# A top-p attention kernel on one core: one bound's trial moved to VectorE, pauses between ScalarE's trials, q in three parts

## The chip, the cores and the metric

The kernel runs on one core of one Trainium2 chip. A core has five engines, each with its own queue of instructions taken in order: TensorE (PE, matrix products), VectorE (DVE), ScalarE (ACT, functions of one input), GpSimd (POOL) and SyncE (SP, here only transfers). Engines wait for each other by semaphores. The metric is the device time of one execution in microseconds (us); lower is better.

## What is computed

A graph layer (layer 0) and an attention layer (layer 1) on 3327 nodes of 256 features. The change lies in layer 1:

```python
def _top_p_attention(X, W1, W2, W3):
    q = X @ W1.T @ W2.T
    k = X @ W3.T
    probs = softmax(q @ k.T)
    idx = argsort(-probs)
    sp = take_along_axis(probs, idx)
    cs = cumsum(sp)
    keep_sorted = cs - sp < 0.9
    mask = zeros(probs.shape).at[rows, idx].set(keep_sorted)
    A = probs * mask
    return A / maximum(A.sum(-1, keepdims=True), 1e-12)

for n in range(2):
    A = _top_p_attention(Xa, W1, W2, W3)
    Xf = R @ Xf
    Xa = A @ Xa
    Z = Z + Xf @ U1[n].T + Xa @ U2[n].T
h = X + Z
return layernorm(h) * ln_g + ln_b
```

R is the neighbours' average with the node itself. For each row the attention keeps the largest probabilities until their sum reaches 0.9.

## The kernel before

**Tiles and items.** The 3327 rows are 26 tiles of 128 (the last has 127). Layer 1 runs 52 items: step 0's tiles, then step 1's; item i covers one tile. An item's product (`product`) is seven groups: `turn` transposes four 128x128 blocks of the masked probabilities on TensorE (L1403) and copies them to SBUF on ScalarE (L1405, `at`); `times` multiplies them with Xa (L1419, `pav`). Between the groups lie seven slots, into which `run` puts the work of other items: logits (L1196, L1199), exponentials, the sorted lists on VectorE, the mask (L1320). `scaled` (L1430) divides by the row's sum. The order of TensorE, ScalarE and VectorE is thus written by hand: an engine takes its instructions in the order in which the calls stand. GpSimd's and SyncE's order is left to a scheduler.

**Extra tiles.** Most rows find their threshold in a sorted list of their 72 largest probabilities. Rows that do not are put aside: `put_aside_1` and `put_aside_2` give them numbers and scatter their index, offset and sum to a table (L1529 on VectorE, L1530 on GpSimd). They are done again in three extra tiles h0, h1, h2 of 128 rows each. For each:

- `hard_load` fetches the rows' numbers (`payh`, L1542 and L1543 cast them) and gathers their features (L1551; in the last item six gathers: three of h2, and the fourth source, Xf after the second step, of each extra tile).
- `hard_q` makes q: transposes (L1180), a copy (L1182, `xtqh`), two matmuls (L1562, `pqh`), a copy (L1564), then a first bound `top` of the threshold (L1570, L1571).
- `hard_exp` makes the probabilities in four pairs of pieces: matmuls (L1581, `plh`) and exponentials (L1584).
- The bound of the threshold is then lowered by up to six trials, at a factor of 1/16, 1/4, 1/2, 0.71, 0.84 and 0.92 (`CUTS`). A trial sums what lies above a candidate and asks whether it still reaches the needed mass. `coarse_bound` does a trial on ScalarE: four activations over half of the row each (L1601), then eight small operations on GpSimd (L1607 to L1616, and L1596 of the next trial). `bound` does one on VectorE: the candidate (L1628), one instruction over 128x3327 (`kept_sum`, L1340), two small ones.
- `hard` sums what lies below the bound (L1643), lists and sorts it, and masks the probabilities (L1672). `hard_end` is the product of the extra tile, in four parts.

**The end.** After the last product, `ends` runs in ticks (`more`). In each tick the next step of an extra tile's product or start is taken, one of the 26 normal tiles' ends is begun (`tile_end`), and every open one goes a stage further: transposes and copies two ticks later (L1180, L1182 `xtut`, `xtvt`), output terms three ticks later (L1439), then the copy (L1447), and two layer norms (L1392 to L1394) and the store. Below, te0 to te25 are these ends; te_k's terms come in tick k + 3. At the close of a tick, the open coarse bounds are given two steps:

```python
            for _ in range(2):
                for g in bounds:
                    if not next(g, True):
                        break
```

Two steps are one pair of activations. `hard(0)` drives ticks 1 to 8, h1's trials on VectorE 9 to 11, `hard(1)` 12 to 19; the product of h0 lies in ticks 9 to 12.

**Where the extra tiles' work stands before.** q of h0 stands in slot 6 of item 48, q of h1 in slot 3 of item 50 (`total` is 52). h0's first trial on ScalarE lies in item 50, its second in the last item, slots 0 and 1; its other four on VectorE in slots 2 to 6 of the last item. h1's first trial on ScalarE lies in slots 3 to 6 of the last item, its second and third in ticks 1 to 4. `start(2)` makes q and the exponentials of h2; its three trials on ScalarE follow in ticks 5 to 10.

Of the kernel before, what the change touches and what calls it, by code (L numbers as in the profile page):

```python
# [17 lines left out]
N = 3327  # L18
# [56 lines left out]
CUTS = tuple(2.0 ** -f for f in (4.0, 2.0, 1.0, 0.5, 0.25, 0.125))  # L75
# [1046 lines left out]
class Layer1:  # L1122
# [432 lines left out]
        )  # L1555

    def hard_q(self, k):
        nc, v = self.nc, self.items[f"h{k}"]
        xt = self.transposed((v.x[:, 0, :],), P, f"q{v.tag}")
        pq = self.psm.tile([P, 512], F32, tag="sm", name=f"pq{v.tag}")  # L1560
        for c in range(DC):
            nc.tensor.matmul(pq[:, :P], self.sh.wq[:, c, :], xt[:, c, :], start=(c == 0), stop=(c == DC - 1))  # L1562
        v.q = self.work.tile([P, DC, P], F32, tag="xtq", name=f"q{v.tag}")[:, 0, :]
        nc.scalar.copy(v.q, pq[:, :P])  # L1564

        v.p = (*self.more, self.p[0])[k]
        v.other = (self.l[0][:, :N], self.l[1][:, :N], self.p[1])[k]

        v.top = self.small(f"top{k}", f"top{v.tag}")
        nc.scalar.activation(v.top, v.pay[:, 3:4], AF.Exp, bias=v.pay[:, 1:2])  # L1570
        nc.gpsimd.tensor_scalar(v.top, v.top, 1.0001, None, ALU.mult)  # L1571
# [14 lines left out]
    def coarse_bound(self, k, cuts, junk):  # L1586


        nc, v = self.nc, self.items[f"h{k}"]
        tag = v.tag  # L1590
        less = self.small(f"less{k}", f"less{tag}")
        nc.gpsimd.tensor_scalar(less, v.pay[:, 2:3], 0.5 * (1.0 - 1e-5), None, ALU.mult)
        for f in cuts:
            tag = f"{v.tag}_{f}"
            minus = self.small(f"minus{k}", f"minus{tag}")
            nc.gpsimd.tensor_scalar(minus, v.top, -f, None, ALU.mult)  # L1596
            s = self.small(f"sums{k}", f"sums4{tag}", 4)
            for h in range(2):
                on = slice(h * HALF, min(N, (h + 1) * HALF))
                for j, func in enumerate((AF.Relu, AF.Sign)):  # L1600
                    nc.scalar.activation(  # L1601
                        junk[:, on], v.p[:, on], func, bias=minus, accum_out=s[:, 2 * h + j : 2 * h + j + 1]
                    )
                    if h == 0 or j == 0:
                        yield
            both = self.small("both", f"both{tag}", 2)
            nc.gpsimd.tensor_tensor(both, s[:, 0:2], s[:, 2:4], ALU.add)  # L1607
            number = self.small("many4", f"many4{tag}")
            nc.gpsimd.tensor_scalar(number, both[:, 1:2], 0.5, 0.5 * N, ALU.mult, ALU.add)
            nc.gpsimd.tensor_tensor(number, number, minus, ALU.mult)  # L1610
            nc.gpsimd.tensor_tensor(number, both[:, 0:1], number, ALU.subtract)
            up = self.small("up4", f"up4{tag}")
            nc.gpsimd.tensor_scalar(up, number, less, f - 1.0, ALU.is_lt, ALU.mult)
            nc.gpsimd.tensor_scalar(up, up, 1.0, None, ALU.add)
            nxt = self.small(f"top{k}", f"top{tag}")
            nc.gpsimd.tensor_tensor(nxt, up, v.top, ALU.mult)  # L1616
            v.top = nxt
            yield

    def bound(self, k, cuts):  # L1620
# [122 lines left out]
    def ends(self, bounds):  # L1743


        ends, open_ends, queue = [self.tile_end(t) for t in range(NT)], [], []

        def tick():

            if ends:  # L1750
                open_ends.append(ends.pop(0))
            for g in list(open_ends):
                if next(g, True):
                    open_ends.remove(g)

        def more():
            if queue and next(queue[0], True):
                queue.pop(0)
            tick()
# [4 lines that stand above are left out]
                        break  # L1764

        def start(k):
            self.hard_q(k)
            for pair in self.chunks():
                yield
                self.hard_exp(k, pair)  # L1770
            bounds.append(self.coarse_bound(k, CUTS[:COARSE], self.items[f"h{k}"].other))

        def end(k):
            yield from self.hard_end(k)
            open_ends.append(self.items[f"h{k}"].end)

        queue.append(start(2))
        for k in range(HARD):
            if k:
                for _ in bounds[k - 1]:  # L1780
                    pass
                for _ in self.bound(k, CUTS[COARSE:]):
                    more()
            for _ in self.hard(k):
                more()
            queue.append(end(k))
        while queue or open_ends or ends:
            more()
        for k in range(HARD):
            self.hard_store(k)  # L1790

    def run(self):
        nc, sh, total = self.nc, self.sh, STEPS * NT
        self.items = {}
        with self.tc.manual_schedule(
# [14 lines left out]
            for i in range(total):  # L1810
# [8 lines left out]
                def slot(g, f, *a):  # L1819
                    slots[g].append(lambda: f(*a))  # L1820
# [28 lines left out]
                if i == NT + CLOSE + 1:  # L1849
                    slot(0, self.hard_load, 0)  # L1850
                    slot(0, self.hard_load, 1)
                if i == total - 4:
                    slot(6, self.hard_q, 0)
                if i == total - 2:
                    slot(3, self.hard_q, 1)
                for k, at, first in ((0, total - 3, 0), (1, total - 2, 3)):
                    if i == at:
                        for j, pair in enumerate(self.chunks()):
                            slot(first + j, self.hard_exp, k, pair)

                if total - 2 <= i:
                    coarse = self.coarse_bound(0, CUTS[i - total + 2 :][:1], self.l[0][:, :N])
                    for g in (0, 1, 2, 3) if i == total - 2 else (0, 0, 1, 1):
                        slot(g, next, coarse, None)
                for k, pair in enumerate(pairs):
                    slot(2 * k, self.some_logits, i + 2, pair, end)
# [1 line left out]
                    slot(g, next, rest, None)  # L1868
                if i + 1 == total:
                    self.put_aside_2(i)  # L1870
                    bound = self.bound(0, CUTS[2:])
                    bounds = [self.coarse_bound(1, CUTS[:COARSE], self.l[1][:, :N])]
                    for g in (2, 3, 4, 5, 6):
                        slot(g, next, bound, None)
                    for g in (3, 4, 5, 6):
                        slot(g, next, bounds[0], None)
                    slot(5, self.hard_load, 2)
                    for k in range(HARD):
                        slot(5, self.hard_gather, k, 3, sh.xf2_rows)
# [100 lines left out]
```

## Time and profile before

| | us |
|---|---|
| three runs | 1853.77, 1857.93, 1858.95 |
| median | 1857.93 |
| the profiled execution | 1861.15 |
| its span from first to last instruction | 1859.1 |
| granted TensorE clock, mean over the span | 0.951 |

Busy time in the span and its share, from the page: PE 1666.4 (90%), DVE 1318.3 (71%), ACT 1031.2 (55%), POOL 1158.7 (62%).

The profile names an instruction by the line of the kernel, its engine and operation, and what it writes and reads, with buffer numbers left out; `x4` counts instructions in a group. A bracket at the end of a line gives the time for which the engine was idle just before, and the instruction that ended this wait. The places in the span that matter here:

| from us | what runs |
|---|---|
| 1585.5 | product of the last item (TensorE) |
| 1602.5 | VectorE's first trial of h0 |
| 1615.3 | h1's second trial on ScalarE; tick 1 |
| 1667.3 | product of h0 begins (tick 9) |
| 1703.4 to 1810.0 | ends of the tiles and product of h1, TensorE in ticks of 5.27 |
| 1818.6 | product of h2, the last one |

### The profile page before, as it was taken

Reading aid. Unit: us, or ns where it says so; the run is one execution under the profiler, and the core shown is the slowest. Engines: PE = TensorE matmul, PEld = TensorE weight load, DVE = VectorE, ACT = ScalarE, POOL = GpSimd, SP = SyncE. Lnnn points to the kernel's source line nnn. Section 1 sums busy time; section 2 is a strip of 40 time slices with the busy share of each in tenths; the row PEclk is TensorE's granted clock in tenths of the full one; section 3 lists DMA queues with packets and bytes.
Section 4 is the critical chain, followed back from the end, with each engine's and each line's share of the span. In section 5 each row is a group of like instructions: output and inputs, shape, how many; then the busy total and the mean of one; then the engine's idle time right before and its main releaser. Section 6 shows DMA issues by size and latency. Waiting matters only on the chain. (4 is left out here: it accounts for less than half of the span.)

```text
span 1859.1 us, 27521 instructions
## 1 busy us (share of the span) xinstructions
PE 1666.4 (90%) x8093; PEld 1221.4 (66%) x8093; DVE 1318.3 (71%) x4095; ACT 1031.2 (55%) x2373; POOL 1158.7 (62%) x1908
## 2 busy tenths in 40 slices
PE   6589999969999999999996999999999988679994
PEld 4355555547777777777774777777777656568873
DVE  5688888456555665655546999999999876585872
ACT  2356666735556555555653555555555446676563
POOL 1578888637886666666654655666666573455754
PEclk9799998979999999999997999999999998889997
DMA  9766664212221111111101111111111120122330
GB/s 313 229 230 212 212 209 119 70 58 76 83 63 43 41 41 40 44 49 46 43 26 40 46 46 49 49 53 55 51 52 49 49 61 20 40 77 89 120 97 29
DMA packets 95099, 154.22 MB, mean 83 GB/s; under 512 B 16471, under 2 KB 68174, under 8 KB 94941
## 3 DMA queue, kind: packets, MB, share of 16 engines
q1 hardware_dynamic: 63818, 86.51, 14.2%
q0 software_dynamic: 20384, 53.28, 11.0%
q10 hardware_dynamic: 10738, 12.58, 2.1%
q8 instruction: 67, 1.10, 0.3%
q14 instruction: 92, 0.75, 0.1%
HBM read 124.65 MB, written 27.75 MB: 82 GB/s over the span
## 5 line engine op out<-in xcount | busy, mean ns | idle before, releaser
L1419 PE MATMUL pav<-xa,at 128*128 128x256 f32 (+2 forms) x1352 | 333.0, 391 | 8.8 <-ACT at L1405 8.8
L1405 ACT COPY at<-pt 128x512 f32<-128x512 f32 (+2 forms) x364 | 192.0, 542 | 262.7 <-PE pt L1403 168.3
L1419 PE MATMUL pav<-x,at 128*128 128x256 f32 (+2 forms) x1352 | 325.7, 385 | 7.9 <-ACT at L1405 7.6
L1419 PEld LDWEIGHTS pav<-xa,at 128*128 128x128 f32 (+2 forms) x1352 | 247.1, 192 | 90.0 <-ACT at L1405 41.8
L1419 PEld LDWEIGHTS pav<-x,at 128*128 128x128 f32 (+2 forms) x1352 | 244.4, 190 | 72.6 <-ACT at L1405 28.5
L1199 ACT COPY array<-pl 128x416 f32<-128x416 f32 (+4 forms) x405 | 183.1, 503 | 182.8 <-PE pl L1196 179.5
L1212 DVE MAX8 cand<-array 128x8 f32<-128x167 f32 (+5 forms) x921 | 239.0, 335 | 48.5 <-ACT array L1199 48.5
L613 POOL DMA_INDIRECT g<-xf_rows,edge x130 | 136.1, 1047 | 160.0 <-PE pxf L1365 127.9
L613 POOL DMA_INDIRECT g<-x_rows,edge x130 | 146.1, 1124 | 103.6 <-PE ptq L626 70.9
L1196 PE MATMUL pl<-kT,qT 64*128 64x416 f32 (+4 forms) x810 | 198.7, 561 | 6.3 <-ACT x L1584 2.7
L1304 DVE TENSOR_TENSOR_SCAN before<-e 128x40 f32<-128x40 f32 (+3 forms) x52 | 14.5, 279 | 227.0 <-ACT e L1297 217.7
L1357 POOL TENSOR_SCALAR m<-col,erow 128x128 f32<-128x128 f32 x260 | 157.0, 618 | 14.4 <-PE pxf L1365 8.0
L613 POOL DMA_INDIRECT g<-whx,edge x130 | 137.6, 1058 | 43.6 <-issue 35.6
L1365 PE MATMUL pxf<-g,m 128*128 128x256 f32 (+1 forms) x520 | 134.7, 408 | 13.2 <-POOL m L1357 6.4
L1365 PEld LDWEIGHTS pxf<-g,m 128*128 128x128 f32 (+1 forms) x520 | 98.6, 199 | 68.8 <-issue 40.7
L1230 DVE MAX8 lst<-cand 128x8 f32<-128x160 f32 (+3 forms) x364 | 114.6, 315 | 9.2 <-issue 0.2
L1403 PE MATMUL pt<-ident,array 128*128 128x128 f32 (+1 forms) x676 | 100.9, 276 | 6.0 <-DVE array L1320 6.0
L819 DVE FIND_INDEX8 at<-ones,array 128x8 uint32<-128x840 f32 (+1 forms) x104 | 105.6, 1027 | 0.0
L1403 PE MATMUL pt<-ident,p 128*128 128x128 f32 (+2 forms) x676 | 100.3, 274 | 4.3 <-DVE p L1320 4.3
L1403 PEld LDWEIGHTS pt<-ident,array 128*128 128x128 f32 (+1 forms) x676 | 84.9, 144 | 24.2 <-PE pxf L1365 7.6
L1403 PEld LDWEIGHTS pt<-ident,p 128*128 128x128 f32 (+2 forms) x676 | 84.7, 144 | 21.6 <-PE pxf L1365 8.0
L1320 DVE SCALAR_TENSOR_TENSOR array<-array,t,array 128x3327 f32<-128x3327 f32 x26 | 96.2, 3699 | 0.5
(467 smaller groups left out, 3321.6 us busy)
## 6 DMA issues: line engine op xcount, KB each, us to landing
array<-in_adj_dram SPq DMA_DIRECT2D x23, 1248.0 KB
array<-in_adj_dram SPq DMA_DIRECT2D x23, 415.5 KB
xf_rows<-xf SPq DMA_DIRECT2D x50, 128.0 KB
xa_rows<-xa SPq DMA_DIRECT2D x50, 128.0 KB
xfs<-xf_rows SPq DMA_DIRECT2D x50, 128.0 KB
whx<-table ACTq DMA_DIRECT2D x25, 129.5 KB
x_rows<-x ACTq DMA_DIRECT2D x25, 128.0 KB
xb_rows<-xb SPq DMA_DIRECT2D x25, 128.0 KB
```

Source lines behind the costliest of these rows:

```text
L613: self.nc.gpsimd.indirect_dma_start(out=dst[:, b, :], out_offset=None, in_=table[:, :], in_offset=bass.IndirectOffsetOnAxis(ap=self.edge[: ...
L819: nc.vector.max_index(at[:r, g, :], self.ones8[:r], ad[:r, g, :])
L1196: nc.tensor.matmul(pl[:r, :w], q[on], self.sh.kT[on, n, s : s + w], start=True, stop=True)
L1199: nc.scalar.copy(l[:r, h * HALF + s : h * HALF + s + w], pl[:r, :w])
L1212: self.nc.vector.max(cand[:r, g * 8 : g * 8 + 8], src[:r, g * group : min(N, (g + 1) * group)])
L1230: nc.vector.max(lst[:r, k : k + 8], cand[:r])
L1320: nc.vector.scalar_tensor_tensor(v.p[:r], v.l[:r, :N], v.t[:r], v.p[:r], ALU.is_ge, ALU.mult, accum_out=sA[:r])
L1357: nc.gpsimd.tensor_scalar(v.m[:, b, :], sh.col1, sh.erow[:, v.at, b : b + 1], None, ALU.is_equal)
L1365: nc.tensor.matmul(acc[:r, :D], v.m[:, b, :r], v.g[:, b, :], start=(b == 0), stop=(b == EB - 1))
L1403: nc.tensor.transpose(pt[: rows(j), j - j0, :r], v.p[:r, cols(j)], self.ident[:r, :r])
L1405: nc.scalar.copy(at[:, :full, :r], pt[:, :full, :r])
L1419: nc.tensor.matmul(v.acc[: v.r, :D], at[:k, j - 4 * g, : v.r], V[:k, j, :], start=(j == 0), stop=(j == NT - 1))
```

## The change

`hard_q` becomes a generator with three parts: transposes and their copy; the matmuls of q and their copy; the first bound. For h0 they stand in slots 4, 5 and 6 of item 48, for h1 in slots 1, 2 and 3 of item 50, and `start(2)` spends two more ticks on h2's. `coarse_bound` yields three times after a trial instead of once, so that in the ticks a pause of one tick lies between two trials. h0's second trial (1/4) moves from ScalarE to VectorE: `bound(0, ...)` has five trials instead of four, in slots 0 to 5 of the last item, and h1's first trial on ScalarE moves from slots 3 to 6 to slots 1 to 4. The changed kernel's lines after L1557 are up to seven higher (L1601 is L1604 there).

```diff
     def hard_q(self, k):
...
         xt = self.transposed((v.x[:, 0, :],), P, f"q{v.tag}")
+        yield
         pq = self.psm.tile([P, 512], F32, tag="sm", name=f"pq{v.tag}")
...
         nc.scalar.copy(v.q, pq[:, :P])
+        yield
 
         v.p = (*self.more, self.p[0])[k]
...
             nxt = self.small(f"top{k}", f"top{tag}")
             nc.gpsimd.tensor_tensor(nxt, up, v.top, ALU.mult)
             v.top = nxt
+
+            yield
+            yield
             yield
...
         def start(k):
-            self.hard_q(k)
+            yield from self.hard_q(k)
             for pair in self.chunks():
...
-                if i == total - 4:
-                    slot(6, self.hard_q, 0)
-                if i == total - 2:
-                    slot(3, self.hard_q, 1)
+                for k, at, first in ((0, total - 4, 4), (1, total - 2, 1)):
+                    if i == at:
+                        q = self.hard_q(k)
+                        for g in range(3):
+                            slot(first + g, next, q, None)
...
-                if total - 2 <= i:
-                    coarse = self.coarse_bound(0, CUTS[i - total + 2 :][:1], self.l[0][:, :N])
-                    for g in (0, 1, 2, 3) if i == total - 2 else (0, 0, 1, 1):
+                if i == total - 2:
+                    coarse = self.coarse_bound(0, CUTS[:1], self.l[0][:, :N])
+                    for g in (0, 1, 2, 3):
                         slot(g, next, coarse, None)
...
-                    bound = self.bound(0, CUTS[2:])
+                    bound = self.bound(0, CUTS[1:])
                     bounds = [self.coarse_bound(1, CUTS[:COARSE], self.l[1][:, :N])]
-                    for g in (2, 3, 4, 5, 6):
+                    for g in (0, 1, 2, 3, 4, 5):
                         slot(g, next, bound, None)
-                    for g in (3, 4, 5, 6):
+                    for g in (1, 2, 3, 4):
                         slot(g, next, bounds[0], None)
```

## The prediction

> **What bounds the kernel now.** I read the share of busy time first (TensorE 90 %, VectorE 71 %, ScalarE 55 %), which says that most of the kernel is TensorE's. The page's chain of waits holds only the last store, so for the stretch that the change touches (the last product and the ends after it) I read, in this order, busy time in windows, the waits between 1570 and 1680 us, and the instructions of each engine there. The windows (time from the start; busy us and count of PE, PE's loads, DVE, ACT, POOL; the clock granted):
>
> ```profile
> 1602.70:1615.30 12.60, 4.33 (x18) 2.53 (x16) 12.18 (x14) 4.02 (x8) 8.94 (x9) 0.81 0.16 43
> 1615.30:1667.30 52.00, 36.13 (x177) 29.06 (x177) 49.31 (x102) 43.67 (x70) 24.08 (x47) 0.86 0.23 69
> 1680.00:1703.40 23.40, 22.37 (x117) 19.27 (x117) 9.49 (x14) 15.86 (x33) 14.66 (x21) 1.00 0.30 96
> 1703.40:1731.00 27.60, 26.41 (x137) 22.51 (x136) 25.75 (x82) 19.77 (x55) 18.71 (x40) 1.00 0.40 120
> 1731.00:1810.00 79.00, 75.96 (x401) 65.48 (x400) 60.16 (x143) 45.75 (x124) 54.62 (x82) 1.00 0.35 107
> ```
>
> Up to 1667 us TensorE is idle a third of the time and ScalarE and VectorE are full; from 1667 to 1810 TensorE is full and ScalarE has slack. The waits of the first part (waiting instruction, what released it; total us, times, longest):
>
> ```profile
> DVE cndh L1628 <- POOL toph_0.25_16249 L1616: 20.0, 1, 20.0
> PE pavh L1419 <- ACT ath L1405: 9.9, 1, 9.9
> PE plh L1581 <- ACT array L1584: 8.6, 1, 8.6
> ACT array L1601 <- POOL minush_0.25_16392 L1596: 7.8, 1, 7.8
> ACT p L1601 <- POOL minush_0.25_16760 L1596: 3.5, 1, 3.5
> ```
>
> VectorE stands 20 us before its first trial of h0, TensorE 9.9 us before the product of h0 because ScalarE's queue is late, and ScalarE 7.8 us before h1's second trial because GpSimd is late. GpSimd's own records say why (start, duration):
>
> ```profile
> 1607.47 3.55 POOL L1613 TENSOR_SCALAR up4h_0.0625_16362<-many4h_0.0625_16358,lessh 128x1 f32<-128x1 f32 x1
> 1611.10 0.22 POOL L1614 TENSOR_SCALAR up4h_0.0625_16362<-up4h_0.0625_16362 128x1 f32<-128x1 f32 x1
> 1611.69 3.59 POOL L1596 TENSOR_SCALAR minush_0.25_16392<-toph_0.0625_16365 128x1 f32<-128x1 f32 x1
> ```
>
> An operation on 128x1 takes 0.2 us, but 3.6 us where it began beside one of VectorE's trials (L1340, 1607.17 to 1610.85 and 1611.53 to 1615.21): it ends only with the trial. Five gathers of L613 begun inside such a VectorE instruction took 2.64 to 4.16 us against a median of 1.00.
>
> **What the skill says.** The Trainium skill's "SBUF — State Buffer", section "Who interferes with whom", says that a VectorE instruction with two SBUF inputs contends with a GpSimd instruction that reads SBUF, and that the second to issue blocks fully until the first ends. The trace agrees (3.55 and 3.59 us above). The page supposes, as inferred, that writing a gather's descriptors isn't held up by the read side alone; the five gathers say that here they are. "TensorE: Matmul & The Clock Gate", section "Part 1: The HAM clock gate", lets idle time lower TensorE's clock. Here eight matmuls of L1419 take 3.78 us after the wait of 9.9 and 1.99 otherwise; four of L1562 take 1.23 after 4.31 idle and 0.71 after 3.46.
>
> **q in three parts.** No instruction is added for h0 and h1; the transposes go earlier in their product. Before, in item 50:
>
> ```profile
> 1570.96 1.23 PE L1562 MATMUL pqh<-xtqh,wq 128*128 128x128 f32 x4 [4.31 <-ACT xtqh L1182]
> 1572.54 1.76 PE L1581 MATMUL plh<-kT,qh 64*128 64x416 f32 x4 [0.35 <-ACT qh L1564]
> ```
>
> With the copy a slot ahead of its matmuls most of 4.31 goes, and the slow groups behind it (0.5 and 0.8 over). I take 5 us for item 50, and 1 for item 48, where the mask on VectorE comes nearly as late as TensorE. So the last product starts near 1580 instead of 1585.5. For h2 the two extra yields put its q and its exponentials two ticks later; its bound is asked for in tick 7 instead of 5.
>
> **The trial moved.** ScalarE loses four activations of 1.68 and four accumulator reads of 0.19 (7.5 us) in the last product, VectorE gains one trial: from one L1340 to the next it is 4.37 us (1602.81, 1607.17, 1611.53). VectorE has 20 us idle there, so the trial is free, and its five start when the first trial's bound comes, near 1580: 1580 + 5 x 4.37 is 1602, the read of the sum (L1643, 3.68 long) then, instead of at 1620.06. VectorE's chain for h0 is some 17 us earlier, The last product took TensorE 17.1 us (1585.54 to 1602.67), 1.5 of it a wait for a copy behind a trial: it ends near 1595.6, ScalarE's trial of h1 and the scaling with it, 7 and 10 us earlier than before (1602.7 and 1605.6).
>
> What is late next is GpSimd. Before, its scatter of the rows put aside (L1530), two casts and six gathers (L1551) ran from 1584 to 1600.5, in VectorE's idle time. Now five trials lie over them, with 0.7 us free between two. One scatter, then a DMA of 3.9, small casts, then about one gather for a trial: near 1605.7, when the sum's instruction ends, I expect three or four gathers left, at 1.3 each 4 to 5 us, and behind them the chain of h1's first trial (L1607 to L1616, then L1596, 2.6 us): minush_0.25 for h1 near 1613 to 1614, against 1615.28. ScalarE, done with h1's first trial early, waits for it. Of the 8 to 17 us won before, 1 or 2 remain here.
>
> **The pauses.** An activation pair takes 3.5 us (2 x 1.68 and the reads). Up to times0 of h0 (1667.26), ScalarE ran eight pairs in ticks 1 to 8: h1's second and third trial, h2's first and second. After, it is h1's in ticks 2, 3, 5, 6 and the first half of h2's in tick 8; h2's others stand in ticks 9, 11, 12, 14, 15. Three pairs, 3 x 3.5 = 10.5, leave the stretch where ScalarE is full, and the wait of 3.5 for minush_0.25 of h2 with them, part of which TensorE's own rate of 5.27 us per tick takes back. With the 1 to 2 from above I take 12 us: times0 near 1655 (bounds 9 and 15).
>
> What is moved costs in its new place, where TensorE is full. ScalarE's slack ahead of what TensorE waits for, before:
>
> ```profile
> 1700.57 0.47 ACT L1430 ACTIVATE xa_h<-pavh,rAh 128x256 f32<-128x256 f32 x1 [0.23 <-PE pavh L1419]
> 1713.18 0.59 ACT L1182 COPY xtut<-ptxut 128x512 f32<-128x512 f32 x1 [0.57 <-PE ptxut L1180]
> 1723.71 0.59 ACT L1182 COPY xtut<-ptxut 128x512 f32<-128x512 f32 x1 [1.70 <-PE ptxut L1180]
> 1728.97 0.59 ACT L1182 COPY xtut<-ptxut 128x512 f32<-128x512 f32 x1 [0.58 <-PE ptxut L1180]
> ```
>
> In the new order the pair of tick 11 stands right ahead of xa_h, behind which TensorE's transposes of h0 wait: 3.5 less 0.23 (and 0.1 of rounding) is 3.2. The pair of tick 12 meets the slack of 0.57: 2.9. Those of 14 and 15 meet 1.70 and 0.58: 1.8 and 2.9. Sum 10.8. The pair of tick 9 falls into the long product ticks (8 to 11 us each, as two of h2's did before) and is free. Each of these waits is near 3 us, and whether TensorE's clock falls there isn't shown: after 2.04 us idle (1540.85) the next group of L1419 took 3.65 instead of 1.99, after 1.52 (1597.86) it did not, and the 0.71 above says that 3.46 need not cost either. Bounds: 0 and three such groups (5); I take one, 1.7. If the slack were better used (3.57 busy of 5.27 in a tick without a pair), the two pairs of ticks 14 and 15 cost 2 x (3.5 - 1.7) = 3.6 rather than 4.7, and those of 11 and 12 half: 7 is the low end.
>
> **Sum.** -12 (times0 earlier) + 10.8 (pairs) + 1.7 (clock) = +0.5 us, against the profiled execution's 1861.15 (span 1859.1 and 2.05 around it). From tick 17 on the two orders are the same, with 8.03 us of TensorE's wait for h2's mask before the last product as before: VectorE's ticks follow TensorE's. The median of the runs is 1857.93 and the profiled one lies 3.2 over it, which is execution to execution; on the median it gives 1858.4, so 1858. A measurement of this kernel tells 0.3 %, 5.6 us, from no change.
>
> **Rivals.** (a) *GpSimd isn't held up so long.* If the gathers slip in between the trials, the chain of h1 ends near 1604, as soon as ScalarE has done the trial. Then times0 comes up to 8 us earlier still, near 1647, until TensorE's own 5.27 per tick bounds; with the low cost of the pairs (7) and no clock loss: -20 + 8 = -12, 1846. For it: ScalarE's and TensorE's work is done in time; against it: 3.55 and 3.59, and the gathers of L613. (b) *The pairs of h2 ahead of xa_h and the tiles' copies outweigh the gain.* Its place is ticks 11 to 16, its price 10.8 and 5 for slow groups; the gain is 9 because minush waits for all six gathers behind the sum's instruction (1616). +7, so 1865. It decides once the gain at times0 is under about 10 us. For it: TensorE is at 96 % in these windows, so nothing there is hidden. (c) *The split and the trial do nothing at all*, as the wait for GpSimd moves with them, and the pauses are worth their own: -9 + 9, again no change; it counts with the forecast.
>
> **The numbers.** No measurable change, with (c): 0.42. Slower, (b): 0.31, which is as likely as my gain at times0 being 4 us too large. Faster, (a): 0.27. The likeliest is 1858, its own range 1852.4 to 1863.5; the range that holds 8 in 10 reaches to the middle of both others: 1847 to 1867.
>
> **What would show it.** Right: VectorE's first trial of h0 near 1580 and L1643 near 1602; gathers of L1551 of 3 to 4 us; ScalarE idle 10 us or more ahead of minush_0.25 of h1, near 1614; times0 of h0 near 1655; waits of about 3 us ahead of xa_h's transposes and of three of the tiles te10 to te14. Wrong: gathers of 1.0 us (then (a)), times0 after 1658 or slow groups behind each wait (then (b)), or a last product that starts no earlier than 1585.

## The result, and the profile after

| | median of 20 runs, us | range | ratio to before, 95 % interval |
|---|---|---|---|
| before | 1858.09 | 1853.77 to 1861.36 | |
| after | 1859.09 | 1853.92 to 1863.87 | 1.0005 [0.9997, 1.0013] |

No measurable change, as forecast (1858). The profiled execution of the changed kernel took 1856.41 us with a span of 1854.6. It is 2.7 us under its median as that of before is 3 us over its own, so positions in the two traces are compared from a common point: the first matmul of L1365 of item 45, at 1421.2 us before and at 1415.9 after. In what follows, "earlier" counts from there (5.3 us are taken off).

Some of the waits between 1560 and 1700 us in the changed kernel: waiting instruction, what released it, total us, times, longest.

```profile
ACT array L1604 <- POOL minush_0.25_16420 L1599: 7.8, 1, 7.8
PE pavh L1419 <- ACT ath L1405: 4.9, 1, 4.9
PE pzt L1439 <- ACT xtut L1182: 8.5, 4, 6.0
PE ptxqh L1180 <- DMA xh<-xa_rows,idxh: 5.2, 1, 5.2
PE ptxwh L1180 <- ACT xa_h L1430: 3.7, 1, 3.7
```

The 20 us of VectorE ahead of its first trial are gone and TensorE's wait ahead of times0 (the first group of the product of h0) is halved. ScalarE waits for GpSimd as long as before, only earlier, and TensorE waits 6.0 for the copies behind it, where before it waited 8.6 for the exponentials behind it. Two waits of TensorE are new: 5.2 for the gathered features of h2, as TensorE gets there earlier and the gather doesn't, and 3.7 ahead of xa_h's transposes. VectorE's first and last step of h0's bound:

```profile
1570.45 0.15 DVE L1634 TENSOR_SCALAR cndh<-toph_0.0625_16115 128x1 f32<-128x1 f32 x1 [0.57 <-POOL toph_0.0625_16115 L1619]
...
1593.01 3.68 DVE L1649 SCALAR_TENSOR_TENSOR array<-x,toph 128x3327 f32<-128x3327 f32 x1
```

The sum's instruction starts 21.8 us earlier than before (1620.06). GpSimd beside it (start, duration):

```profile
1584.88 4.33 POOL L1551 DMA_INDIRECT xh<-xa_rows,idxh  x1 [0.16 <-POOL thrh L1631]
1589.51 3.89 POOL L1551 DMA_INDIRECT xh<-x_rows,idxh  x1 [0.30 <-issue]
1593.70 3.87 POOL L1551 DMA_INDIRECT xh<-xf_rows,idxh  x1 [0.30 <-issue]
1597.87 0.99 POOL L1551 DMA_INDIRECT xh<-xf_rows,idxh  x1 [0.30 <-issue]
1599.17 1.00 POOL L1551 DMA_INDIRECT xh<-xf_rows,idxh  x1 [0.31 <-issue]
1600.47 0.99 POOL L1551 DMA_INDIRECT xh<-xf_rows,idxh  x1 [0.30 <-issue]
...
1603.59 0.21 POOL L1599 TENSOR_SCALAR minush_0.25_16420<-toph_0.0625_16323 128x1 f32<-128x1 f32 x1
```

Each of the first three gathers begins inside a VectorE instruction (L1340, L1340, L1649) and ends 0.88 to 1.05 us after that one has ended, which is about what an undisturbed gather takes. Three are left when the sum is done, and h1's chain comes behind them. Ahead of the gathers the trials also held two other operations: L1371 took 2.88 us for 0.73 before, the cast L1542 2.23 for 0.18. Two groups of TensorE before, then TensorE in the changed kernel from times0 of h0 on (the bracket is the wait ahead of a group; most lines without a wait worth naming are left out):

```profile
1701.10 0.44 PE L1180 MATMUL ptxwh<-ident,xa_h 128*128 128x128 f32 x2 [0.56 <-ACT xa_h L1430]
...
1713.82 1.99 PE L1439 MATMUL pzt<-u,xtut 128*128 128x256 f32 x8 [0.24 <-ACT xtut L1182]
```

```profile
1646.78 3.78 PE L1419 MATMUL pavh<-xa,ath 128*128 128x256 f32 x8 [4.86 <-ACT ath L1405]
...
1683.93 0.69 PE L1180 MATMUL ptxwh<-ident,xa_h 128*128 128x128 f32 x2 [3.69 <-ACT xa_h L1430]
1685.08 2.07 PE L1439 MATMUL pzh<-u,xtwh 128*128 128x256 f32 x4 [0.46 <-ACT xtwh L1182]
...
1701.77 2.62 PE L1439 MATMUL pzt<-u,xtut 128*128 128x256 f32 x8 [3.02 <-ACT xtut L1182]
1704.19 2.99 PE L1439 MATMUL pzt<-u,xtvt 128*128 128x256 f32 x8
...
1715.66 2.85 PE L1439 MATMUL pzt<-u,xtut 128*128 128x256 f32 x8 [1.92 <-ACT xtut L1182]
...
1723.71 1.99 PE L1439 MATMUL pzt<-u,xtut 128*128 128x256 f32 x8 [1.34 <-ACT xtut L1182]
```

times0 starts at 1646.78 instead of 1667.26, 15.2 us earlier by the common point. Then come the four waits that the prediction named, where before TensorE waited 0.56 ahead of xa_h's transposes and 0.24 in a tick, and slower groups behind three of them. At te14's terms the kernel is 0.6 us ahead of before, and stays there. The windows say the same (columns as in the prediction; the last two are the DMA share and GB/s):

```profile
1646.80:1680.20 33.40, 33.40 (x166) 29.02 (x166) 12.20 (x23) 17.30 (x41) 20.27 (x34) 0.93 0.20 64
1680.20:1726.00 45.80, 34.89 (x150) 28.70 (x150) 31.11 (x90) 34.55 (x76) 23.20 (x59) 0.85 0.31 95
1726.00:1805.00 79.00, 75.67 (x399) 64.90 (x397) 57.99 (x137) 45.56 (x123) 53.68 (x80) 1.00 0.33 99
```

TensorE is busy 34.9 of 45.8 us in the stretch where h2's pairs stand, at a granted clock of 0.85; before it was busy 26.41 of 27.60 in the same ticks (1703.40 to 1731.00), at 1.00.

### The profile page after: what moved, and what is told of

The parts are those of the page before. It is cut to its first block, busy times and chain, and to the rows that moved or that the text cites. A ratio compares the mean times of both kernels' runs of the same rounds, so it can differ in the third digit from the quotient of the medians.

```text
span 1854.6 us, 27513 instructions
## 1 busy us (share of the span) xinstructions
PE 1666.1 (90%) x8093; PEld 1222.6 (66%) x8093; DVE 1324.8 (71%) x4100; ACT 1023.9 (55%) x2365; POOL 1165.0 (63%) x1899
## 5 line engine op out<-in xcount | busy, mean ns | idle before, releaser
L1419 PE MATMUL pav<-xa,at 128*128 128x256 f32 (+2 forms) x1352 | 329.1, 388 | 7.0 <-ACT at L1405 7.0
L1212 DVE MAX8 cand<-array 128x8 f32<-128x167 f32 (+5 forms) x921 | 239.0, 335 | 43.7 <-ACT array L1199 43.7
L1365 PE MATMUL pxf<-g,m 128*128 128x256 f32 (+1 forms) x520 | 132.7, 403 | 13.4 <-POOL m L1357 6.8
L1365 PEld LDWEIGHTS pxf<-g,m 128*128 128x128 f32 (+1 forms) x520 | 97.4, 196 | 68.8 <-issue 41.3
```

The source lines that it names most:

```text
L1212: self.nc.vector.max(cand[:r, g * 8 : g * 8 + 8], src[:r, g * group : min(N, (g + 1) * group)])
L1365: nc.tensor.matmul(acc[:r, :D], v.m[:, b, :r], v.g[:, b, :], start=(b == 0), stop=(b == EB - 1))
L1419: nc.tensor.matmul(v.acc[: v.r, :D], at[:k, j - 4 * g, : v.r], V[:k, j, :], start=(j == 0), stop=(j == NT - 1))
```

## The experiments

My theory: what comes earlier ahead of times0 of h0 is real, and h2's pairs of activations, moved into ticks where TensorE is full, give it back pair by pair. Rivals: the earlier work is swallowed by a wait (GpSimd's, or ScalarE's full queue) and the pauses alone move anything; or the loss behind times0 has another cause than where the pairs stand. The table shows each kernel's place relative to before, in us from the common point in its own profiled execution (minus is earlier), and its time. Item 51 is the first matmul of L1365 ahead of the last product; all other columns are TensorE's groups. Each row is one execution. Kernels whose code is the same up to item 50 differ there by up to 2.2 us, and e10_notrial lies 3.1 to 5.3 us behind the others with the split, so differences of 2 to 3 us in one row say little.

| kernel | item 51 | times0 of h0 | te8 | te14 | te25 | median, us (before beside it) | ratio to before |
|---|---|---|---|---|---|---|---|
| after | -8.8 | -15.2 | -15.0 | -0.6 | -0.6 | 1859.09 (1858.09) | 1.0005 [0.9997, 1.0013] |
| e1_split | -7.1 | -9.2 | -9.5 | -1.9 | -1.9 | 1860.64 (1860.44) | 1.0004 [0.9996, 1.0012] |
| e2_trial | -1.2 | -1.8 | -1.5 | -1.5 | -1.5 | 1861.11 (1860.44) | 0.9998 [0.9990, 1.0006] |
| e3_pause | -1.5 | -6.2 | -5.6 | +9.0 | +8.9 | 1869.48 (1860.44) | 1.0048 [1.0035, 1.0061] |
| e4_nopause | -8.5 | -13.0 | -13.5 | -4.3 | -4.3 | 1859.20 (1860.44) | 0.9991 [0.9981, 1.0001] |
| e5_single | -7.4 | -15.0 | -17.2 | -12.3 | -7.3 | 1853.21 (1860.73) | 0.9958 [0.9945, 0.9971] |
| e6_h2whole | -7.4 | -4.8 | -5.7 | -5.6 | -5.7 | 1856.16 (1860.73) | 0.9976 [0.9965, 0.9986] |
| e7_gathers | -6.6 | -9.1 | -8.8 | -8.8 | -8.8 | 1851.80 (1860.73) | 0.9958 [0.9944, 0.9972] |
| e8_single_g | -7.5 | -18.9 | -21.2 | -16.2 | -11.2 | 1849.18 (1860.73) | 0.9951 [0.9932, 0.9969] |
| e9_steps | -7.2 | -19.4 | -21.7 | -16.6 | -16.6 | 1842.43 (1856.76) | 0.9930 [0.9916, 0.9943] |
| e10_notrial | -3.5 | -11.3 | -11.9 | -5.1 | -3.5 | 1850.83 (1856.76) | 0.9962 [0.9947, 0.9978] |

### One part alone, and the pauses taken away

e1_split is before with the new `hard_q` and its slots, e2_trial with h0's second trial moved, e3_pause with the pauses alone, e4_nopause is after without them:

```diff
             v.top = nxt
-
-            yield
-            yield
             yield
```

> The kernel before with only the split of q (all three tiles). Theory (the gain before the product of h0 is real, and h2's pairs that land in ticks 11 to 16 give it back, pair by pair): the last product starts about 8 us earlier; VectorE still stands idle before its first trial, and minush_0.25 of h1 comes 7 to 9 us earlier; h2's pairs stand in ticks 7 to 12, so six instead of eight lie ahead of times0 of h0, which begins 12 to 15 us earlier; the pairs of ticks 11 and 12 cost 5 to 7 after it. Median 1850 (1847 to 1853). Rival (whatever comes earlier ahead of times0 is swallowed by a wait further on, and only the pauses move times0): 1856 to 1860.

> The kernel before with only h0's second trial on VectorE and h1's first trial in slots 1 to 4. Theory: VectorE is done with h0's trials 10 to 14 us earlier, but GpSimd's gathers are held by the trials, so that minush_0.25 of h1 comes 0 to 4 us earlier; ScalarE's eight pairs lie ahead of times0 as before, nothing is added behind it: 1855 (1852 to 1858). Rival (VectorE or ScalarE is what bounds up to times0, GpSimd is not): 1845 to 1850.

> The kernel before with only the pauses. The pairs stand in the same ticks as in the changed kernel (2, 3, 5, 6, 8, 9, 11, 12, 14, 15). Theory: times0 of h0 comes 6 to 10 us earlier, the pairs of ticks 11 to 15 cost about 14: slower, 1863 (1860 to 1867). Rival (the pauses are what gains, and the loss in ticks 11 to 16 is of another cause): 1848 to 1853.

> The changed kernel without the pauses: h1's pairs in ticks 1 to 4, h2's in 7 to 12. Theory: one pair more ahead of times0 (up to 3.5 us later than in the changed kernel), two pairs instead of four behind tick 10, so of the 14.6 us given back 6 to 7 remain: faster than both, 1853 (1850 to 1856). Rival (the pauses carry the gain ahead of times0): slower than the changed kernel, 1863 or more.

The signs of the moves are the theory's, most sizes are not, and of the four times only that of e3_pause came out on the theory's side, beyond its range (1860 to 1867): e1_split (1850 expected), e2_trial (1855) and e4_nopause (1853) cannot be told from the kernel before. The split alone starts the last product 7 us earlier and times0 9.2 earlier (12 to 15 expected), and its two late pairs of ticks 11 and 12 give back 7.6: nothing that the runs can tell is left, as the rival's number had it, though the gain was not swallowed ahead of times0 but lost behind it. The trial alone moves nothing, as GpSimd's chain for h1 is not earlier (minush_0.25 at 1613.56, and ScalarE's trial behind it 0.6 earlier than before by the common point). The pauses alone gain 6.2 and lose 15: 9 us slower, and the rival that they are what gains falls. Without them the changed kernel gives back 9.2 instead of 14.4 from te8 to te14, but has 2 us less to give, and 9.2 is more than the 6 to 7 expected of two pairs: half of e4's loss comes from the pair of tick 11 and a slow group behind it (4.1, te8 to te9).

### The same activations in other ticks

e6_h2whole makes h2's q in one tick, so that its pairs stand in ticks 5 to 10 as before; e5_single gives the bounds one step per tick:

```diff
-            yield from self.hard_q(k)
+            for _ in self.hard_q(k):
+                pass
...
-            for _ in range(2):
+            for _ in range(1):
                 for g in bounds:
```

(the first three lines are e6_h2whole's, the others e5_single's; neither has pauses.)

> Split of q and the trial on VectorE as in the changed kernel, no pauses, and each tick gives the bounds one step instead of two: ScalarE gets one activation (1.87 us) per tick, h1's eight in ticks 1 to 8, h2's twelve from tick 9 on. Theory (a pair costs what it exceeds ScalarE's slack by, and more where the wait that it leaves TensorE is near 3 us): an activation alone meets slack of 0.57 to 1.7, so a wait is at most 1.4 and no group is slow after it; times0 of h0 13 to 18 us earlier than before, 4 to 8 given back: 1850 (1846 to 1854), against 1858 to 1860 before. Rival (the sum of ScalarE's work in the full ticks decides, not its portions): as much given back as in the changed kernel, 1858 or more.

> The changed kernel without pauses and with h2's q made in one tick, as before; so all ten pairs stand in ticks 1 to 10, as in the kernel before, and only what comes earlier in items 48 to 51 is left. Theory: times0 of h0 comes 6 to 9 us earlier than before, nothing is given back after it: faster than before by 6 to 9, that is 1851 to 1854. Rival (ScalarE's eight pairs ahead of times0 swallow what came earlier): as before.

Both came out on the theory's side. e6_h2whole keeps its 5.7 us from te8 to the end: without pairs behind tick 10 nothing is given back; at times0 it has 4.8, less than the 6 to 9 expected, and its time is 4.6 us under that of before. e5_single has ten activations of h2 behind tick 10, the changed kernel eight, but in e5_single they come one by one except the last two. TensorE in e5_single, in ticks with an activation:

```profile
1685.54 0.44 PE L1180 MATMUL ptxwh<-ident,xa_h 128*128 128x128 f32 x2 [1.89 <-ACT xa_h L1430]
1686.44 2.08 PE L1439 MATMUL pzh<-u,xtwh 128*128 128x256 f32 x4 [0.46 <-ACT xtwh L1182]
...
1700.86 1.99 PE L1439 MATMUL pzt<-u,xtut 128*128 128x256 f32 x8 [1.21 <-ACT xtut L1182]
...
1717.62 1.99 PE L1439 MATMUL pzt<-u,xtut 128*128 128x256 f32 x8 [1.22 <-ACT xtut L1182]
...
1737.99 3.44 PE L1419 MATMUL pavh<-xa,ath 128*128 128x256 f32 x8 [3.94 <-ACT ath L1405]
```

The waits are 1.2 to 1.9, and the tiles' groups behind those of 1.2 keep their 1.99. That no group would be slow did not hold: behind the wait of 1.89 `pzh` took 2.08 us for 1.13, at a granted clock of 0.60 from 1686.4 to 1690.6. Between te8 and te14 e5_single loses 4.9 us for five activations where the changed kernel loses 14.4 for eight. What is lost after te14 (5 us) is the last line: h2's last two activations are done together ahead of h1's product, and the group behind that wait is slow too. In all, these ten activations cost 9.9 us, the eight in pairs 14.4.

### GpSimd's gathers

e7_gathers is e6_h2whole, and e8_single_g is e5_single, with the gathers of the fourth source behind h1's chain; their index is made again with a bound that depends on h1's second candidate and changes no value (shortened; the calls lie in a generator of the end's ticks):

```diff
-                    for k in range(HARD):
-                        slot(5, self.hard_gather, k, 3, sh.xf2_rows)
...
+                self.nc.gpsimd.tensor_scalar(
+                    v.idx[:, 1:2], v.pay[:, 0:1], float(N - 1), minus, ALU.min, ALU.max
+                )
+                self.hard_gather(k, 3, self.sh.xf2_rows)
```

> The same as e6_h2whole, and three of the six gathers (the fourth source of each extra tile) wait for h1's second candidate, so that they stand behind h1's chain on GpSimd. Theory (GpSimd's gathers hold back h1's second trial and with it ScalarE's queue): minush_0.25 of h1 3 to 4 us earlier, times0 2 to 4 us earlier, the time 2 to 4 us less than e6_h2whole. Rival (ScalarE's pairs or TensorE's own rate bound these ticks): the same as e6_h2whole within 1 us.

> e5_single with the three gathers behind h1's chain. Theory: with one activation per tick ScalarE waits less for the chain, so this brings less than in e7_gathers: 0 to 3 us less than e5_single. Rival (GpSimd's chain bounds whatever stands behind it): 3 to 4 us less.

ScalarE's wait for h1's second trial in e6_h2whole, and then in e7_gathers:

```profile
1610.07 1.68 ACT L1603 ACTIVATE array<-x,minush_0.25_16380 128x1664 f32<-128x1664 f32 x1 [9.66 <-POOL minush_0.25_16380 L1598]
```

```profile
1605.96 1.68 ACT L1604 ACTIVATE array<-x,minush_0.25_16371 128x1664 f32<-128x1664 f32 x1 [5.78 <-POOL minush_0.25_16371 L1598]
```

Three gathers less, 3.9 us less wait, and it arrives in full: times0 4.3 earlier, 4.4 us off the median (3.3 by the ratios). For e8_single_g the profiled executions show the same gain over e5_single (3.9 at times0 and at te25), and the medians 4.0, which is what the rival said; but its runs scatter from 1846.1 to 1857.2, the ratios differ by 1.3 us only, and their intervals overlap. So in the traces GpSimd's chain bounds this stretch with single activations too, and what this is worth in time isn't settled by these runs. The wait for this chain is the one that the change leaves as long as it found it (7.8).

### Putting it together

```diff
+        steps = iter([1] * 8 + [2] * 2)
...
-            for _ in range(1):
+            for _ in range(next(steps, 1)):
                 for g in bounds:
```

> e8_single_g with two activations instead of one in ticks 9 and 10, the long ticks of h0's product, so that h2's last ones stand in tick 18 and none are left to be done together ahead of h1's product. Theory: the wait of 3.9 us ahead of h1's product and the slow group behind it (5 us in all) go, the two activations more cost nothing in ticks of 8 to 11 us: 3 to 5 us less than e8_single_g, 1844 to 1847. Rival (those ticks are as full as the others): 1849 or more.

> e9_steps with h0's second trial back on ScalarE in the last product, as in the kernel before. Theory (the last product and GpSimd, not VectorE, set when h1's second trial starts; moving the trial frees ScalarE and costs GpSimd): 0 to 4 us more than e9_steps, up to 1850. Rival (VectorE's earlier end carries the gain up to times0): 8 us more or worse, 1853 and up.

e9_steps is faster than both kernels: 0.9930 [0.9916, 0.9943] of before, some 13 us. It ran on another chip than e8_single_g, where the kernel before took 4 us less, so its 1842 is not to be set against the expected 1844 to 1847; the ratios put it 3.9 us under e8_single_g, within the 3 to 5 expected, though their intervals overlap. Loss and slow group ahead of h1's product are gone. It is also the plainest comparison of portions: eight activations of h2 lie behind tick 10, as in the changed kernel, but one by one, and from te8 to the end they cost 5.1 us instead of 14.4. (Of the 14.4, 5.9 are slow groups, of which e9_steps has none in these ticks; without them it is 5.1 against some 8.5.) TensorE's waits for ScalarE from 1640 to 1735 us (total us, times, longest):

```profile
PE pzt L1439 <- ACT xtut L1182: 5.4, 7, 3.1
PE pavh L1419 <- ACT ath L1405: 2.3, 2, 2.0
PE ptxwh L1180 <- ACT xa_h L1430: 1.9, 1, 1.9
```

The 3.1 is where one of h2's activations waits (1.96 us) for GpSimd's chain between two trials and holds the tiles' copies behind it. A pause might help there; no run tried it.

With the trial back on ScalarE (e10_notrial) it is 8.4 us slower by the medians and 6 by the ratios, more than the theory's 0 to 4 and near the rival's 8. So the trial, which moves nothing by itself (e2_trial), is worth 6 to 8 us here. Its profiled execution (1856.29) is the slowest of its seven, so its row counts for little, but it shows who holds GpSimd's chain:

```profile
1605.51 3.60 POOL L1598 TENSOR_SCALAR minush_0.25_16375<-toph_0.0625_16356 128x1 f32<-128x1 f32 x1
```

VectorE's trials, which wait for the second trial's bound, lie over h1's chain and hold two of its operations (3.56 and 3.60 us for 0.2 to 0.3), as in the kernel before. So moving the trial takes VectorE's work off GpSimd's chain and lays it over the gathers. Where the 6 to 8 us come from isn't shown by this: minush_0.25 comes 4.7 us later than in e9_steps, but 3.7 of these were lost by item 50, where the two kernels are still the same.

## Why the prediction was right

The time came out as the sum did, +0.5 forecast and -0.6 in the trace, and the path was the forecast one. But three terms were off by 2 to 4 us and cancelled: 3.2 us more were won, the pairs cost 2.1 less and the clock 4.2 more. Two of them, the gain and the clock, lie past the bounds that the prediction gave them. That the sum came so near is in part luck.

- **Split of q.** I had the last product 6 us earlier. It is 8.8 in the changed kernel and 6.6 to 7.5 in e5 to e8, which do not differ there. The wait of 4.31 ahead of L1562 became 0.28. The term was somewhat small.
- **The trial.** That it is free for VectorE, and that GpSimd is late next, held. I had the first trial begin where GpSimd's chain would come near 1580; with 5.3 taken into account it came at 1575.8, and the sum's instruction at 1598.3, not 1602.
- **GpSimd.** Three gathers of 3.9 to 4.3 us, three left behind: as worked out. But all of it lay earlier with the trials, and minush_0.25 was ready 6.2 us earlier than before (1603.80 against 1611.69 + 3.59 - 5.3), where I had 1 to 2. ScalarE waited 7.8 for it, not 10 or more.
- **times0 of h0.** 15.2 us earlier, for 12 with bounds of 9 and 15. What GpSimd gave was more. On the way TensorE lost some of it again, which I had not put in: te1 was 15.3 earlier, te5 10.2. Of these 5.1 us some 3 are slow groups of te1 behind the wait of 6.0 for ScalarE, and about 1 is a wait behind h1's pair of tick 6. The wait ahead of times0, 4.9 instead of 9.9, gave 5 back.
- **The pairs behind it.** 3.2, 2.9, 1.8 and 2.9 were worked out; over the wait of a tick in the kernel before (0.56 ahead of xa_h's transposes, 0.24 else) the trace has 3.1, 2.8, 1.7 and 1.1, 8.7 in all. The last was too high; that TensorE was late by then and ScalarE had more slack is my reading, not tested.
- **The clock.** I took one slow group, 1.7, of 0 to 5. It was 5.9, past the upper bound: 14.6 us lost less 8.7 of waits, and the groups show them: two transposes 0.69 for 0.44, `pzh` 2.07 for 1.13 and 1.06 for 0.59, then the tiles' groups 2.66, 2.62, 2.99, 2.85 and 2.76 where it was 1.89 to 1.99. The granted clock was 0.50 to 0.58 in these places (1683.9 to 1689.7: 0.53; 1703.2 to 1707.0: 0.58; 1717.0 to 1720.0: 0.50). This term is of one execution and can differ in another, as e1_split and e4_nopause show:

```profile
1711.79 1.99 PE L1439 MATMUL pzt<-u,xtut 128*128 128x256 f32 x8 [2.96 <-ACT xtut L1182]
```

```profile
1710.28 2.69 PE L1439 MATMUL pzt<-u,xtut 128*128 128x256 f32 x8 [2.96 <-ACT xtut L1182]
1712.76 2.92 PE L1439 MATMUL pzt<-u,xtvt 128*128 128x256 f32 x8
```

Both kernels have a wait of 3.70 ahead of xa_h's transposes and one of 2.96 that ends 17.1 us later; behind the second, the first kernel's groups are at full speed and the second's are slow.

So the gain went as forecast: won ahead of times0, given back in ticks 12 to 17. Of rival (a), GpSimd's chain was earlier than I thought, but not for its reason: the gathers did not slip in between the trials. (In its sum 8 us stand for the pairs, where its text names 7.) Of (b), the price of slow groups came (5.9 for its 5). Of (c), the trial by itself and the split by itself do move nothing measurable, but the pauses, worth nothing on balance there, cost 9 us alone. What is left open is why the clock falls behind some of these waits and not behind others as long.

## What to carry to other kernels

A piece of work moved out of a full stretch is paid for in the place that receives it: read that place's slack per period and compare it with the size of the portion, not with its sum over the stage. Here eight activations in portions of 3.5 us against a slack of 0.2 to 1.7 gave back 14.4 of 15 us, and eight in portions of 1.9 us gave back 5.1. Before an engine's work is moved beside another's, look for who is locked out there: the same trials held two small operations of h1's chain in one place and three gathers in the other.

## What the runs showed of the hardware

Indirect gathers on GpSimd took 3.87 to 4.33 us instead of 0.99 when they began inside a VectorE instruction of 3.68 us with two inputs in SBUF (L1340, L1649), and ended 0.88 to 1.05 us after it; 128x1 operations of 0.2 us took 3.55 to 3.60. Beside VectorE's MAX8 (L1212) three gathers took 0.99 to 1.00. Which part of a gather is held isn't shown.

The length of TensorE's waits does not decide whether its clock falls. Behind a wait of 2.96 us that ended 17.1 after one of 3.70, a group took 1.99 us in e1_split and 2.69 in e4_nopause. Behind 1.89, `pzh` took 2.08 in e5_single and 1.13 in e9_steps. A wait of 3.10 in e9_steps was followed by 1.99, one of 1.92 in the changed kernel by 2.85. What does decide stays open.
